# Placing each value of a planned four-layer graph kernel in the buffer that the plan names

## The chip, the cores and the metric

The kernel runs on one core of a Trainium2 chip. A core has engines that work in parallel, each with its own queue of instructions: TensorE (PE, matrix products and transposes; its weight loads are listed apart as PEld), VectorE (DVE), ScalarE (ACT), GpSimd (POOL), and SyncE (SP), which here issues all the DMA transfers. Values lie in SBUF (128 partitions) and, where TensorE writes, in PSUM (8 banks); inputs, the output and a few intermediates lie in HBM. Engines wait for each other through semaphores.

The metric is the device time of one execution in microseconds (us), lower is better. The median of three runs of the kernel before is 2722.01 us (2721.93 to 2723.06).

## The reference

64 graphs of 256 nodes with 256 features, `x` (64, 256, 256), go through four layers, each with the dense weighted adjacency `adj` (64, 256, 256). After each layer comes a residual and a normalisation over the features. Shortened, for one graph, in float32:

```python
# layer 0: 4 heads, sigmoid attention, normalised by the degree
X, q, k = heads(lrelu(x @ W_lin + b_lin)), heads(lrelu(x @ W_q)), heads(lrelu(x @ W_k))
A = adj * sigmoid(q @ k.T * 64 ** -0.5)
deg = A.sum(-1);  dis = where(deg > 0, deg ** -0.5, 0)
x = ln(x + affine_ln((dis[:, None] * A * dis[None, :]) @ X))
# layer 1: 8 heads, softmax attention where adj > 0
s = where(adj > 0, q1 @ k1.T / sqrt(32), NEG)
x = ln(x + heads_joined(softmax(s) @ v1) @ Wo + bo)
# layer 2: sum over neighbours, MLP of width 1024 with an RMS norm and SiLU
h = (eps * x + adj @ x) @ W1 + b1
x = ln(x + silu(h * rsqrt(mean(h ** 2) + 1e-6) * rms_weight) @ W2 + b2)
# layer 3: additive attention, softmax, layer norm, GELU
Wh = x @ W;  e = leaky_relu(s1[:, None] + s2[None, :], 0.2)
x = ln(x + gelu(affine_ln(softmax(where(adj > 0, e, NEG)) @ Wh)))
```

## The kernel before, in words

The program is straight-line code made from a plan. `graph()` (L296) describes one graph's work as a list of operations on named values, for 64 graphs; `weights()` (L225) does the same for the constants. An `Op` (L54) has an engine, an estimated cost, a function that issues its instructions, and the values that it writes and reads. A `Value` (L42) has a kind, which says what it lies in: `s` (128 x 516 words of SBUF, most values), `d` (128 x 1024, the attention weights `e`, `eb`, `eT`), `b` (128 x 2048, `att` and `hT`), `c` (128 x 32, statistics), `p` (one PSUM bank) and `h` (HBM, `far`). `SLOTS` (L39) says how many of each there are at a time: 42, 10, 3, 72, 8 and 8.

`Plan.order()` (L143) is a list scheduler in plain Python that runs when the program is built. It keeps a clock for each engine, takes the operation that can start first, and for each of its new values takes a slot: `self.free[kind]` holds pairs of the time from which a slot is free and its number; it is sorted, and the first is taken (L199, L200). When the last use of a value has been placed, its slot goes back with the time at which that use has landed (L203 to L205). An operation that needs more slots than are free waits until there are enough. So the plan has a slot number, `v.slot`, for each value; but the number goes no further than the plan's own clock. The result is one list, sorted by the planned start (L217), in which operations of up to eight graphs stand beside each other: layers 1, 2 and 3 of a graph run 2, 5 and 7 graphs behind layer 0 (`ROUND`, L37).

`emit()` (L787) goes through that list. It asks a pool for a tile for each value that an operation is the first to use, then issues the operation. Each kind has one pool with as many buffers as `SLOTS` says (L761), and all its tiles have one tag, so the framework beneath decides which of the free buffers a tile gets, by its own account of when each becomes free, and makes the first writer of a tile wait for all readers of the tile that lay there. The framework keeps each engine's instructions in the order in which they are issued (L783); it adds all semaphores.

The steps that the prediction speaks of:

- L434 (VectorE), `y = ps + xb`, the residual after layers 1 and 2, where `ps` comes from L377 or L695; then statistics L391, L393, on POOL L403 and L404, then L414 (VectorE, two numbers per row) and L418 (ScalarE), which makes the next `x1`, `x2` or `x3`.
- L321 (TensorE), the transposes of such an `x`; L377 and L366, products of 256 columns in both layouts.
- L502 (VectorE), `added`, the sum of two halves of `att` (layer 0); L508 (TensorE) sums it over nodes for the degrees; L530 (TensorE) multiplies `att` by the values `v0`.
- L606 (TensorE), `av`, layer 1's attention times `v1`; L623 (VectorE), `yT = av * rb`, where `rb` are the softmax's reciprocals, which come by way of L615 (`rT`, ScalarE), a write to HBM (L616) and eight reads (L619).
- L654 and L656 (ScalarE), `sq` and `hT` of layer 2; L661 and L663 (VectorE) add the `sq`, L668 (TensorE) takes their mean; L695 is the last product of layer 2.
- L333, L339, L343: a transpose by way of HBM (VectorE in blocks, four writes of `far`, four reads), which gives `xT3` (read by L710) and `eT3` (read by L377) in layer 3.

Of the kernel before, what the change touches and what calls it, by code (L numbers as in the profile page):

```python
# [9 lines left out]
F32 = mybir.dt.float32  # L10
# [3 lines left out]
P = 128  # L14
# [15 lines left out]
WORDS = {"s": 516, "d": 1024, "b": 2048, "c": 32, "p": 512, "h": 1024}  # L30
# [8 lines left out]
SLOTS = {"s": 42, "d": 10, "b": 3, "c": 72, "p": 8, "h": 8}  # L39
# [700 lines left out]
@with_exitstack  # L740
def gnn_stack_kernel(ctx: ExitStack, tc: tile.TileContext, t: dict, out: bass.AP):

    nc = tc.nc  # L750
    x_in, xT_in, adj_in, adjT_in = t["x"], t["xT"], t["adj"], t["adjT"]
    B, N, D = x_in.shape
    NB, DB = N // P, D // P
    assert NB == 2 and DB == 2
    H0, H1 = 4, 8
    HD0, HD1 = D // H0, D // H1
    HID = t["L2_gnn_W1"].shape[1]
    HB = HID // P

    const = ctx.enter_context(tc.tile_pool(name="const", bufs=1))  # L760
    pools = {kind: ctx.enter_context(tc.tile_pool(name=f"pool_{kind}", bufs=SLOTS[kind], **(  # L761
        {"space": {"p": bass.MemoryType.PSUM, "h": bass.MemoryType.DRAM}[kind]} if kind in "ph" else {})))
        for kind in SLOTS}


    ident = const.tile([P, P], F32, name="ident")
    make_identity(nc, ident)
    ones = const.tile([P, 32], F32, name="ones")
    nc.vector.memset(ones, 1.0)
    mean_of = const.tile([P, 32], F32, name="mean_of")  # L770
    nc.vector.memset(mean_of, 1.0 / HID)
    mhalf = const.tile([P, 8], F32, name="mhalf")
    nc.vector.memset(mhalf, -0.5)
    c = SimpleNamespace(const=const, ident=ident, ones=ones, mean_of=mean_of, mhalf=mhalf)

    plan = Plan(B)
    weights(plan, nc, c, t)
    for b in range(B):
        plan.graph = b
        graph(plan, nc, c, t, out, b)  # L780
    engines = {mybir.EngineType.PE, mybir.EngineType.DVE, mybir.EngineType.Activation, mybir.EngineType.Pool,
               mybir.EngineType.SP}
    with tc.manual_schedule(engines=engines):  # L783
        emit(plan, pools)


def emit(plan, pools):  # L787
    for op in plan.order():
        for v in op.takes:
            v.full = pools[v.kind].tile([P, WORDS[v.kind]], F32, tag=v.kind, name=v.name)  # L790
            v.t = v.full[:, :512] if v.kind == "s" else v.full
        op.fn()

# [30 lines left out]
```

## Time and profile before

| | us |
|---|---:|
| median of three runs | 2722.01 |
| lowest, highest | 2721.93, 2723.06 |
| the profiled execution | 2723.49 |
| its span, first to last instruction | 2721.6 |
| TensorE busy | 2673.4 |
| VectorE busy | 2441.1 |
| ScalarE busy | 2226.4 |
| GpSimd busy | 595.7 |

The profile is one execution, recorded by the hardware. Busy time is the time in which an engine has an instruction in work. The time from one instruction's start to the next tells more on TensorE, whose instructions overlap. "L502 <- PE L530" in the chain of waits means that the engine sat idle before an instruction of line 502 and that the semaphore which came last was TensorE's, from an instruction of line 530. Which engine or transfer ended a wait is in the profile; whether it was waited for because of a value or because of the room to write to is not, and has to be read from the code. The granted clock of TensorE was 0.996 of full speed over the span, and the 16 DMA engines were busy two thirds of the time (66.2% for the transfers of SP's queue).

### The profile page before, as it was taken

How to read it: one execution, taken by the hardware profiler on the slowest of the kernel's cores; microseconds unless marked ns; L12 is line 12 of the kernel's file. 1: busy time of each engine (PE TensorE's matmuls, PEld its weight loads, DVE VectorE, ACT ScalarE, POOL GpSimd, SP SyncE). 2: the span in 40 equal slices, each digit the busy share in tenths (PEclk: the TensorE clock that was granted, in tenths of full speed). 3: DMA queues.
4: the chain of work that ended last, by engine and by line, in shares of the span. 5: the costliest groups of instructions: out<-in, count | busy, mean ns of one | idle time of the engine just before them, and what ended most of it. 6: DMA issues, size and time to landing. Idle time of an engine off the chain costs nothing.

```text
span 2721.6 us, 56595 instructions
## 1 busy us (share of the span) xinstructions
PE 2673.4 (98%) x17568; PEld 2145.6 (79%) x17568; DVE 2441.1 (90%) x7486; ACT 2226.4 (82%) x5331; POOL 595.7 (22%) x902
## 2 busy tenths in 40 slices
PE   8999999999999999999999999999999999999997
PEld 6777788787887877877878778787778788787776
DVE  6788999899899998999989999989999899999986
ACT  4988788888887888878888788888888888887885
POOL 1111222212222212212222222222222222222212
PEclk9999999999999999999999999999999999999998
DMA  5476876776666766767767677676676676766661
GB/s 150 135 212 176 208 217 164 204 197 183 191 187 181 214 180 181 199 172 208 203 164 206 182 190 213 161 196 193 173 215 188 170 212 184 190 209 177 173 169 38
DMA packets 708045, 501.01 MB, mean 184 GB/s; under 512 B 309792, under 2 KB 667552, under 8 KB 707744
## 3 DMA queue, kind: packets, MB, share of 16 engines
q1 hardware_dynamic: 707744, 497.40, 66.2%
q8 instruction: 140, 2.29, 0.4%
q14 instruction: 161, 1.32, 0.2%
HBM read 301.35 MB, written 195.82 MB: 183 GB/s over the span
## 4 chain that ended last, share of the span: by engine, by line
PE 88%; DVE 4%; ACT 3%; DMA 2%; SPq 1%; issue 1%; POOL 0%; DVEq 0%; POOLq 0%; ACTq 0%
PE ps L366 16%; PE ps L377 15%; PE ps L695 15%; PE ps L649 15%; PE ps L570 5%; PE ps L490 4%; PE ps L530 4%; PE ps L637 4%; PE ps L710 4%; PE av L606 4%; PE ps L321 1%; PE ps L508 1%; ACT e L458 1%; PE pr L681 1%; DVE st L391 1%
## 5 line engine op out<-in xcount | busy, mean ns | idle before, releaser
L458 ACT ACTIVATE e<-e,low 128x256 f32<-128x256 f32 x1152 | 574.7, 500 | 85.2 <-DVE low L453 84.2
L695 PE MATMUL ps<-w,hT 128*128 128x256 f32 x2048 | 466.8, 380 | 1.3 <-ACT hT L687 1.3
L649 PE MATMUL ps<-aggT,w 128*128 128x256 f32 x2048 | 463.4, 380 | 1.6 <-ACT aggT L357 1.0
L695 PEld LDWEIGHTS ps<-w,hT 128*128 128x128 f32 x2048 | 385.7, 190 | 60.4 <-issue 4.6
L649 PEld LDWEIGHTS ps<-aggT,w 128*128 128x128 f32 x2048 | 383.3, 190 | 57.0 <-issue 3.2
L403 POOL TENSOR_SCALAR mv<-mv 128x2 f32<-128x2 f32 x384 | 132.8, 346 | 1347.7 <-DVE mv L393 977.5
L453 DVE CUSTOM_DVE_ANT_0 e<-ps,adj 128x256 f32<-128x256 f32 x1024 | 361.7, 419 | 24.2 <-PE ps L570 24.0
L404 POOL TENSOR_TENSOR mv<-mv,mhalf 128x2 f32<-128x2 f32 x384 | 308.5, 803 | 32.0
L591 DVE STREAM_TRANSPOSE eb<-e 128x1024 f32<-128x1024 f32 x248 | 301.1, 1222 | 0.8 <-ACT e L458 0.7
L656 ACT ACTIVATE hT<-ps,br,r 128x256 f32<-128x256 f32 x512 | 256.0, 585 | 35.0 <-PE ps L695 31.8
L418 ACT ACTIVATE x<-y,mv 128x256 f32<-128x256 f32 x384 | 215.2, 599 | 55.3 <-DVE mv L414 51.6
L654 ACT ACTIVATE sq<-ps,b 128x256 f32<-128x256 f32 x512 | 220.1, 474 | 27.5 <-PE ps L649 23.4
L391 DVE BATCH_NORM_STATS2 st<-y 128x6 f32<-128x256 f32 x640 | 239.0, 410 | 1.2
L458 ACT ACTIVATION_READ_ACCUMULATOR e<-e,low 128x1 f32 x1152 | 219.1, 190 | 0.0
L496 DVE TENSOR_TENSOR att<-att,adjT 128x512 f32<-128x512 f32 x256 | 166.9, 678 | 8.9 <-ACT att L494 8.9
L676 POOL TENSOR_TENSOR rs<-rs,mhalf 128x2 f32<-128x2 f32 x64 | 45.7, 713 | 527.1 <-DVE rs L674 521.6
L516 POOL TENSOR_TENSOR dp<-dp,mhalf 128x8 f32<-128x8 f32 x64 | 109.8, 1715 | 214.6 <-DVE dp L515 168.4
L685 DVE TENSOR_TENSOR hT<-hT,pr 128x1024 f32<-128x1024 f32 x128 | 150.0, 1211 | 5.3 <-PE pr L681 4.5
L570 PE MATMUL ps<-kT,qT 32*128 32x256 f32 x2048 | 148.2, 400 | 0.0
L661 DVE TENSOR_TENSOR sq<-sq 128x512 f32<-128x512 f32 x192 | 130.0, 677 | 13.0 <-ACT sq L654 12.0
L366 PE MATMUL ps<-x0T,w_q 128*128 128x256 f32 x512 | 130.4, 385 | 6.3 <-DMA x0T<-in_xT 6.3
L494 ACT ACTIVATE att<-ps 128x512 f32<-128x512 f32 x256 | 132.2, 602 | 3.9 <-PE ps L490 3.2
(114 smaller groups left out, 5515.5 us busy)
## 6 DMA issues: line engine op xcount, KB each, us to landing
far<-eb SPq DMA_DIRECT2D x248, 512.0 KB, 3.6
eT<-far SPq DMA_DIRECT2D x992, 128.0 KB, 4.1
adj<-in_adj SPq DMA_DIRECT2D x128, 256.0 KB, 5.0
far<-eb SPq DMA_DIRECT2D x488, 64.0 KB, 2.0
x0T<-in_xT SPq DMA_DIRECT2D x64, 256.0 KB, 4.6
adjT<-in_adjT SPq DMA_DIRECT2D x64, 256.0 KB, 5.1
x<-in_x SPq DMA_DIRECT2D x64, 256.0 KB, 5.2
adj<-in_adjT SPq DMA_DIRECT2D x64, 256.0 KB, 4.7
```

Of the source, the lines that this page charges most:

```text
L366: pe.matmul(two(ps)[:, o, :], w.t[:, k, o * P:(o + 1) * P], two(xT)[:, k, :], start=(k == 0), stop=(k == DB - 1))
L377: pe.matmul(two(ps)[:, n, :], two(xT)[:, k, n * P:(n + 1) * P], w()[:, k, :], start=(k == 0), stop=(k == DB - 1))
L391: op("DVE", 328, lambda n=n: dve.bn_stats(st.t[:, 6 * n:6 * n + 6], two(src)[:, n, :]), [(st, n)], [(src, n)])
L404: pool.tensor_tensor(m()[:, :, 2], m()[:, :, 2], c.mhalf[:, :NB], OP.pow)
L453: op("DVE", 345, lambda n=n: dve.tensor_tensor_reduce(out=E(n), in0=two(logits)[:, n, :], in1=two(negmask)[:, n, :], scale=-scale, scalar= ...
L458: op("ACT", 491, lambda n=n: act.activation(E(n), E(n), AF.Exp, bias=low.t[:, n:n + 1], scale=-1.0, accum_out=r.t[:, col(n):col(n) + 1]), ...
L570: pe.matmul(two(pss[i])[:, n, :], two(qT1)[s, hq, n * P:(n + 1) * P], two(kT1)[s, hq, :], start=True, stop=True)
L591: op("DVE", 1155, lambda e=e, eb=eb: dve.transpose(eb.t.rearrange("p (b g i) -> p g b i", b=4, i=32), e.t.rearrange("p (g b i) -> p g b i" ...
L649: pe.matmul(two(ps)[:, i, :], c.w2_1.t[:, k, (j + i) * P:(j + i + 1) * P], two(aggT)[:, k, :], start=(k == 0), stop=(k == DB - 1))
L654: op("ACT", 357, lambda ps=ps, sq=sq, i=i, j=j: act.activation(two(sq)[:, i, :], two(ps)[:, i, :], AF.Square, bias=c.b2_1.t[:, j + i:j + i ...
L656: op("ACT", 491, lambda ps=ps, i=i, j=j: act.activation(Hb(j + i)[:, 0], two(ps)[:, i, :], AF.Identity, bias=c.br2.t[:, j + i:j + i + 1], ...
L695: pe.matmul(two(ps)[:, n, :], Hb(j)[:, 0, n * P:(n + 1) * P], c.w2_2.t[:, j, :], start=(j == 0), stop=(j == HB - 1))
```

## The change

Each pool now gives out single buffers, one for each tag, and the tag holds the plan's slot number. So there are 42 tags `s0` to `s41`, ten `d0` to `d9`, and so on; a value lies in the buffer whose number the plan gave it, and its first writer waits for the readers of the value that had this number before. The number of buffers of each kind and their sizes stay as they are.

```diff
-    pools = {kind: ctx.enter_context(tc.tile_pool(name=f"pool_{kind}", bufs=SLOTS[kind], **(
+    pools = {kind: ctx.enter_context(tc.tile_pool(name=f"pool_{kind}", bufs=1, **(
         {"space": {"p": bass.MemoryType.PSUM, "h": bass.MemoryType.DRAM}[kind]} if kind in "ph" else {})))
         for kind in SLOTS}
...
 def emit(plan, pools):
+
     for op in plan.order():
         for v in op.takes:
-            v.full = pools[v.kind].tile([P, WORDS[v.kind]], F32, tag=v.kind, name=v.name)
+            v.full = pools[v.kind].tile([P, WORDS[v.kind]], F32, tag=f"{v.kind}{v.slot}", name=v.name)
             v.t = v.full[:, :512] if v.kind == "s" else v.full
         op.fn()
```

## The prediction

> **What bounds the kernel now.** First the page's busy times.
>
> ```profile
> PE 2673.4 (98%) x17568; PEld 2145.6 (79%) x17568; DVE 2441.1 (90%) x7486; ACT 2226.4 (82%) x5331; POOL 595.7 (22%) x902
> ```
>
> TensorE sets the end. A busy PE is not yet a full one, so I looked at the distance from matmul to matmul: 215 to 216 ns for each 256-column record, hardly ever more. What can be won is the idle time between them: PE is busy 91.3 of the first 100 us, 2480.8 of the 2500 us after it (the table by stretches), and idle 20.7 us of the end. The middle loses 19.2 us, and that is all a change of buffers can give there. Next the chain of waits for PE alone: waiter, what ended the wait, us in total, times, longest.
>
> ```profile
> PE ps L366 <- DMA x0T<-in_xT: 6.3, 1, 6.3
> PE ps L321 <- ACT x L418: 5.6, 10, 1.0
> PE ps L377 <- DVE mv L393: 2.9, 10, 0.4
> PE ps L321 <- DVE y L434: 2.3, 5, 0.5
> PE ps L508 <- DVE added L502: 2.2, 5, 0.4
> PE ps L668 <- DVE sq L663: 1.8, 1, 1.8
> ```
>
> The first is the start's load. The next four are one pattern: six small stalls, 2.6 us together, that return every 334 us (8 graphs) between 534 and 2036 us, five times over. Why is the engine that PE waits for late? The waits of VectorE tell it:
>
> ```profile
> DVE y L434 <- PE av L606: 11.3, 9, 1.6
> DVE yT L623 <- PE ps L530: 9.7, 7, 1.5
> DVE added L502 <- PE ps L377: 9.6, 5, 1.9
> DVE added L502 <- PE ps L530: 5.8, 5, 1.2
> DVE added L502 <- DMA out<-o: 3.2, 1, 3.2
> ```
>
> None of these five is for data. L502 adds two halves of `att`; L434 adds `ps` (of L695 or L377) and `xb`; L623 multiplies `av` and `rb`. The releaser is each time the last reader of whatever lay in the buffer that the result is written to: the waits are for room. One of them in order of time (start, duration, in brackets the idle time before):
>
> ```profile
> 864.35 0.42 DVE L663 TENSOR_TENSOR sq<-sq 128x256 f32<-128x256 f32 x1
> 865.58 0.69 DVE L434 TENSOR_TENSOR y<-ps,xb 128x512 f32<-128x512 f32 x1 [0.81 <-PE av L606]
> 867.43 0.69 DVE L502 TENSOR_TENSOR added<-att 128x512 f32<-128x512 f32 x1 [1.17 <-PE ps L530]
> ```
> ```profile
> 868.18 0.43 PE L508 MATMUL ps<-added,ones 128*32 128x128 f32 x8 [0.44 <-DVE added L502]
> 868.54 0.66 PE L321 MATMUL ps<-ident,x 128*128 128x128 f32 x4
> 869.59 1.75 PE L377 MATMUL ps<-w_o,yT 128*128 128x256 f32 x7 [0.40 <-DVE mv L393]
> ```
>
> VectorE waits 1.98 us for room, and PE then 0.84 us for VectorE.
>
> **What the Trainium skill says.** Perfetto Trace Analysis, Optimization Strategy: a gap that repeats on the engine that should be saturated can mean that there is not enough SBUF or PSUM for the next tile. The five returns agree, with one difference: room there was, only not the room that was picked. Perfetto Trace Analysis, Tensor Engine Instruction: ACT and DVE are strict FIFO. The trace agrees: whatever stands behind a held L502 starts after it. The same page, Identifying Dependency Chains: an instruction that waits on several engines gets semaphore instructions ahead of it; so another set of waits changes their number. SBUF — State Buffer, "SBUF: two separate sides": between engines only the GpSimd/Vector port is shared. So a value's place should not change an operation's time; no run here shows it yet.
>
> **The change part by part.** Nothing is computed differently, and each engine's order is written out by the plan, so every instruction and DMA keeps its place in its queue. What moves is which value lies where, hence who waits for whose last reader. (1) *Which takeovers change.* The plan hands out the slot that by its clock has been free longest (the sorted `free` list in `order`). I listed its slots and set the trace's times beside them. Of 7491 takeovers in SBUF and PSUM, 2345 get another former value: 1429 in pool s, 326 in d, 377 in p, 213 in c, none in b. The `far` values (h) lie in HBM; by the plan's slots the closest reuse leaves 15.6 us, so they cost nothing.
>
> (2) *What goes.* The stalls with the plan's former value:
> - 868.18 and 869.59: y takes over from an xb last read at 859.91, `added` from an aggT last read at 860.19. y can start at 864.69 (the operation before is done), `added` at 865.30 and end at 866.0; its matmul wants it at 867.74. yT follows `added` by 1.36 us as now: 866.66 to 867.3, wanted at 868.75. Both stalls go: 0.84 us.
> - 948.64 and 950.31: y waits from 946.2 to 947.80; its new slot is free since 944.20. It ends at 946.9, wanted at 948.17; yT, held next by the end of av at 947.8, ends at 948.5, wanted at 949.66. 0.65 us.
> - 1033.82 and 1034.3: `added` waits from 1030.1 to 1032.03 for the reader of a yT; its new slot (an adj) is free since 1024.91. The small mv of L414 behind it, now at 1032.98, can start at 1031.05, ACT's L418 after the two hT at 1031.33, and the halves of x1 end by 1031.9 and 1032.4; PE wants them at 1032.86. 0.96 + 0.17 = 1.13 us.
>
> Sum 2.61 us, five times: 13.0 us, which is also the sum of the four rows (5.6 + 2.9 + 2.3 + 2.2). The L668 row comes once, at 2466 us: ACT's sq at 2460.11 stood 1.91 us for the write of rT to HBM; its new slot, a qT1, is free since 2457.30, before ACT gets there at 2458.1. 1.8 us. Together 14.8 us.
>
> (3) *What is added.* In the unchanged trace only six takeovers would come before the last read of the former value, by 0.00 to 1.95 us, 3.99 us in all. Four are SP's `eT` transfer (L343) at 699.84, 1033.73, 1366.79 and 1701.09, after an xb that L434 reads: this L434 stands behind the held L502 of the last stall, so it moves 1.9 us earlier, and more than the 0.00 to 1.02 us needed. Were that cover gone, SP would hold, and the `rb`, `far` and `eT` transfers behind it; these four `eT` are used 5.2 to 6.1 us after they land. One is an `rb` piece at 292.98 (1.95 us; first use 23.7 us after landing). One is ACT's kT1 at 2451.52 (0.41 us, with L570 a microsecond away). Taken as nothing; the other end is all 3.99 us on PE.
>
> (4) *Waits.* PE's own semaphore instructions will differ in number. The 16 matmuls of L490 take 1.62 us with none, one or two of them in between, those of L570 0.77 us: nothing. On DVE (972 now) one shows 21 to 50 ns; a hundred more or fewer are 5 us of DVE, which idles 280: nothing on PE.
>
> (5) *Stalls that stay*: 4.4 us of the middle (hT at 207.5, yT by DMA at 181.1, xT at 1133, 1801 and 2135, some singles), which take the same slots or wait for data; the start and the end.
>
> The profiled execution took 2723.5 us, of which 1.9 lie outside its span of 2721.6; minus 14.8 that is 2708.7. The median of the runs is 1.5 us below it: 2722.0 - 14.8 = 2707.2.
>
> **The rivals.** *No wait goes* (8%): the waits I read as room are ordering that stays, or the slots picked come out alike: 2722. For it only that the releasers are inferred; against it that the code gives L502 nothing to read from L377 or L530.
>
> *Another wait takes the place* (10%): behind the stalls at 1033.8 stands ACT's L656, idle 35 us in all for hT, whose three buffers rotate as before. If it holds x1 by more than the 0.9 us to spare, those 5.65 us stay: 2712.8. If PE, earlier by 2.6 us a period, also meets its `xT` (L710), which lands as little as 0.25 us ahead of use, half of the rest goes too: 2717.4, within what can be told.
>
> *Slower* (6%): the plan's clock is not the chip's. Once the stalls go, transfers come earlier, and SP, one queue, may be held for room where I see none. The price is 1.02 us (the worst of the four) at one `eT`; the `xT` transfers behind it have 0.25 us, so 0.77 us reach PE per graph. Held in 26 graphs it eats 14.8 + 5.4 us and is slower; in all 61: 2707.2 + 47 = 2754. Against it: four holds in 61, none ahead of a tight xT.
>
> **How the numbers follow.** A kernel like this one, with runs within 1.1 us, can tell about 0.2% (5.4 us): below 2716.6 is faster, above 2727.4 slower. My forecast has 76%: from 2702 (the last 4.4 us of the middle go too) to 2713. With the first part of the second rival this fills 2702 to 2716.5, 81%. Faster 0.82 (forecast and that part); same 0.12 (no wait goes, or most gain is given back); slower 0.06.
>
> **What would show it.** Right: the four rows of PE's waits fall from 13.0 to under 3 us, L668's goes, L502's waits for PE (15.4 us) disappear, as do those of L434 for av; PE busy stays 2673 in a span of about 2707; hT's 35 us on ACT stay. Wrong: new rows for SP at L343 with DVE L434, or PE waiting at L710 or L377 for `eT`; or per-operation times that moved with the addresses.

## The result, and the profile after

The changed kernel takes 2696.15 us (median of six runs, 2694.70 to 2699.38) where the kernel before takes 2721.76 us beside it (six runs, 2718.05 to 2723.06). The ratio is 0.9909, with a 95% interval of 0.9896 to 0.9922. A second set of runs (`after_again`), with the kernel before on the same chip, gave 2698.15 against 2721.07: 0.9917 (0.9902 to 0.9932). The change makes the kernel 23 to 26 us faster. The forecast was 2707.2 us: the direction is right, and the gain is nearly twice the one forecast; the time lies below the range.

The profiled execution of the changed kernel took 2699.38 us. Its page begins so (span; busy time, share and instructions of each engine):

```profile
span 2697.6 us, 56490 instructions
...
PE 2664.2 (99%) x17568; PEld 2144.8 (80%) x17568; DVE 2440.3 (90%) x7486; ACT 2224.6 (82%) x5331; POOL 591.5 (22%) x902
```

Every engine executes as many instructions as before; the whole program has 105 fewer, which are semaphore instructions. The span fell by 24.0 us, from 2721.6 to 2697.6. Two subtractions from this page and the one before split it. The time in which PE is *not* busy, span less PE, fell from 48.2 to 33.4 us: 14.8 us. But PE's *busy* time fell too, from 2673.4 to 2664.2 us, for the same 17568 matmuls: 9.2 us. The forecast has the first part and not the second.

The waits of PE in the changed kernel (waiter, what ended the wait, us in total, times, longest):

```profile
PE ps L366 <- DMA x0T<-in_xT: 6.6, 1, 6.6
PE ps L366 <- ACT xT L357: 1.4, 1, 1.4
PE ps L695 <- ACT hT L687: 1.3, 2, 1.1
PE ps L649 <- ACT aggT L357: 1.0, 2, 0.7
PE ps L710 <- ACT xT L357: 1.0, 1, 1.0
PE ps L649 <- DVE low L453: 1.0, 2, 0.6
PE ps L321 <- ACT e L458: 1.0, 2, 0.7
PE ps L710 <- DMA xT<-far: 0.8, 1, 0.8
```

The rows L377 for mv, L321 for y and L508 for added of the five-fold pattern and the row of L668 are gone, the row L321 for x fell from 5.6 to 0.2 us (one wait near the end), and only waits that occur once or twice are left. VectorE's waits show why. `added` (L502) no longer waits for anything. What y and yT wait for is now the matmul whose result they read (besides the rows below, L695 for y, and one wait of 0.5 us for an `rb` transfer):

```profile
DVE yT L623 <- PE av L606: 19.9, 16, 2.5
...
DVE y L434 <- PE ps L377: 10.9, 14, 1.7
```

The stall that the prediction followed instruction by instruction (864 to 870 us before) lies at 858 to 864 us now. VectorE and then PE, in order of time:

```profile
857.98 0.41 DVE L663 TENSOR_TENSOR sq<-sq 128x256 f32<-128x256 f32 x1
858.32 0.68 DVE L434 TENSOR_TENSOR y<-ps,xb 128x512 f32<-128x512 f32 x1
858.92 0.68 DVE L502 TENSOR_TENSOR added<-att 128x512 f32<-128x512 f32 x1
```
```profile
861.08 0.65 PE L508 MATMUL ps<-added,ones 128*32 128x128 f32 x16
861.66 0.66 PE L321 MATMUL ps<-ident,x 128*128 128x128 f32 x4
862.15 1.89 PE L377 MATMUL ps<-w_o,yT 128*128 128x256 f32 x8
```

VectorE has no bracket (no idle time) left, `added` ends 1.5 us before its matmul starts, and the sixteen L508 are one uninterrupted group. Now take the distance between two starts instead of the brackets. The first eight L508 of the kernel before:

```profile
867.32 0.43 PE L508 MATMUL ps<-added,ones 128*32 128x128 f32 x8
```

From there to L377 at 869.59 it was 2.27 us. Now it is 861.08 to 862.15: 1.07 us. So 1.20 us came back, where the brackets showed 0.44 + 0.40 = 0.84. The difference is 0.18 us for each of the two stalls. This is the first sign of what the forecast missed.

### The profile page after: what moved, and what is told of

Read it like the earlier page. It is cut to its first block, busy times and chain, and to the rows that moved or that the text cites. A ratio compares the mean times of both kernels' runs of the same rounds, so it can differ in the third digit from the quotient of the medians.

```text
span 2697.6 us, 56490 instructions
## 1 busy us (share of the span) xinstructions
PE 2664.2 (99%) x17568; PEld 2144.8 (80%) x17568; DVE 2440.3 (90%) x7486; ACT 2224.6 (82%) x5331; POOL 591.5 (22%) x902
## 4 chain that ended last, share of the span: by engine, by line
PE 94%; DVE 2%; ACT 2%; DMA 1%; issue 0%; SPq 0%; POOL 0%; POOLq 0%; DVEq 0%; ACTq 0%
PE ps L366 16%; PE ps L695 16%; PE ps L377 16%; PE ps L649 15%; PE ps L570 5%; PE ps L490 4%; PE ps L530 4%; PE av L606 4%; PE ps L710 4%; PE ps L637 4%; PE ps L321 1%; PE ps L508 1%; PE pr L681 1%; PE ps L719 0%; DVE e L453 0%
## 5 line engine op out<-in xcount | busy, mean ns | idle before, releaser
L695 PE MATMUL ps<-w,hT 128*128 128x256 f32 x2048 | 466.8, 380 | 1.3 <-ACT hT L687 1.3
L649 PE MATMUL ps<-aggT,w 128*128 128x256 f32 x2048 | 463.4, 380 | 2.0 <-ACT aggT L357 1.0
L695 PEld LDWEIGHTS ps<-w,hT 128*128 128x128 f32 x2048 | 385.7, 190 | 60.4 <-issue 4.6
L649 PEld LDWEIGHTS ps<-aggT,w 128*128 128x128 f32 x2048 | 383.3, 190 | 57.4 <-issue 2.5
L453 DVE CUSTOM_DVE_ANT_0 e<-ps,adj 128x256 f32<-128x256 f32 x1024 | 361.7, 419 | 30.3 <-PE ps L570 30.1
L656 ACT ACTIVATE hT<-ps,br,r 128x256 f32<-128x256 f32 x512 | 256.1, 586 | 34.3 <-PE ps L695 31.1
L418 ACT ACTIVATE x<-y,mv 128x256 f32<-128x256 f32 x384 | 215.1, 600 | 27.3 <-DVE mv L414 25.2
L570 PE MATMUL ps<-kT,qT 32*128 32x256 f32 x2048 | 145.7, 399 | 0.0
L366 PE MATMUL ps<-x0T,w_q 128*128 128x256 f32 x512 | 130.4, 385 | 6.6 <-DMA x0T<-in_xT 6.6
```

Of the source, the lines that this page charges most:

```text
L366: pe.matmul(two(ps)[:, o, :], w.t[:, k, o * P:(o + 1) * P], two(xT)[:, k, :], start=(k == 0), stop=(k == DB - 1))
L453: op("DVE", 345, lambda n=n: dve.tensor_tensor_reduce(out=E(n), in0=two(logits)[:, n, :], in1=two(negmask)[:, n, :], scale=-scale, scalar= ...
L570: pe.matmul(two(pss[i])[:, n, :], two(qT1)[s, hq, n * P:(n + 1) * P], two(kT1)[s, hq, :], start=True, stop=True)
L649: pe.matmul(two(ps)[:, i, :], c.w2_1.t[:, k, (j + i) * P:(j + i + 1) * P], two(aggT)[:, k, :], start=(k == 0), stop=(k == DB - 1))
L656: op("ACT", 491, lambda ps=ps, i=i, j=j: act.activation(Hb(j + i)[:, 0], two(ps)[:, i, :], AF.Identity, bias=c.br2.t[:, j + i:j + i + 1], ...
L695: pe.matmul(two(ps)[:, n, :], Hb(j)[:, 0, n * P:(n + 1) * P], c.w2_2.t[:, j, :], start=(j == 0), stop=(j == HB - 1))
```

## The experiments

Where an experiment's lines are numbered otherwise than the changed kernel's, the text says so. Ratios are to the kernel before on the same chip. Unless it is said, a kernel computes all of the reference.

### Does naming the buffers do anything by itself?

`e1_named_as_before`: one named buffer per number, as in the changed kernel, but a table gives each value the buffer in which it lay before.

```diff
...
     for op in plan.order():
         for v in op.takes:
+            if v.kind in PLACED:
+                v.slot, count[v.kind] = ord(PLACED[v.kind][count[v.kind]]) - 48, count[v.kind] + 1
             v.full = pools[v.kind].tile([P, WORDS[v.kind]], F32, tag=f"{v.kind}{v.slot}", name=v.name)
```

> Every value has a named buffer, as in the change, but the buffer is the one that the kernel before gave it. Theory A (the gain is the placement alone: who waits for whose last reader): the time is that of the kernel before, 2722 us within 5, with the same five-fold pattern of stalls and 'DVE added L502 <- PE ps L377' near 9.6 us. Theory B (named buffers help by themselves, through fewer semaphores or a simpler wait): below 2710 us.

Measured: 2720.69 us, ratio 0.9997 (0.9990 to 1.0003). The four rows of the pattern are those of the kernel before (L668 waits 1.1 us here, and 1.8 us before):

```profile
PE ps L321 <- ACT x L418: 5.6, 10, 1.0
PE ps L377 <- DVE mv L393: 2.9, 10, 0.4
PE ps L321 <- DVE y L434: 2.3, 5, 0.5
PE ps L508 <- DVE added L502: 2.2, 5, 0.4
```

The form of the pools is worth nothing that these times can tell. The gain lies in which value takes over from which. Here too the program has 56595 instructions, as before: their number follows the placement, not the names. That leaves a rival, that fewer semaphore instructions make the gain; two runs further down speak against it. `e6_just_freed` has 56851 instructions, 256 more than the kernel before, and is 18 us faster than it; `e3_all_but_s` has 56548, 47 fewer, and is no faster.

### Which pool carries it?

`e2_s_only` names the buffers of pool s alone; `e3_all_but_s` names those of d, b, c, p and h, and leaves s pooled. The edit of e2 (e3 has "dbcph" for "s"):

```diff
-bufs=1, **(
+bufs=1 if kind in "s" else SLOTS[kind], **(
...
-tag=f"{v.kind}{v.slot}"
+tag=f"{v.kind}{v.slot}" if v.kind in "s" else v.kind
```

> Plan's slots in pool s alone; in d, b, c and p the framework picks from a shared pool, as before. Theory A (the false waits of y, added and yT, all in pool s): nearly the whole gain, 2694 to 2702 us. Theory B (a part of the gain beyond the predicted 14.8 us comes from PSUM slots, p, where L570 waited 2 us at 296 us): about 10 us of it missing, 2704 to 2710 us.

> The complement: plan's slots in d, b, c and p, a shared pool for s. Theory A: 2717 to 2724 us, nothing gained beyond a few us. Theory B (PSUM slots matter): 2708 to 2714 us.

Measured: s alone 2702.19 us, 0.9918 (0.9902 to 0.9935); all but s 2721.36 us, 0.9993 (0.9984 to 1.0001), with the same four rows of PE waits as before, 5.6, 2.9, 2.3 and 2.2 us. So pool s carries the gain, within the interval all of it, and the 916 takeovers that differ in d, c and p are worth nothing without it that the times can tell (e3's trace lacks two stalls of PE near 208 us, 1.3 us together). s alone brings one new row of several waits, six times at most 0.4 us, which the whole change doesn't have:

```profile
PE ps L377 <- ACT rT L615: 2.3, 6, 0.4
```

### Is it the three values that were held?

`e4_three_only`: the placement of before, except that y, added and yT of pool s get a buffer that by the plan has been free for over 1 us, the one that is next needed latest (and the two buffers swap their later values). Of the 7491 takeovers in SBUF and PSUM 115 differ from before.

```diff
...
+        if v.name not in ("y", "added", "yT"):
+            continue
...
+        room = [i for i, u in holds.items() if ends[u] < n and u.end < order[n].start - 1000]
+        if room:
+            best, own = max(room, key=lambda i: then.get(i, 1 << 30)), at[v]
+            for _, u in takes[j:]:
+                at[u] = {best: own, own: best}.get(at[u], at[u])
...
```

> The placement of the kernel before, except that the values named y, added and yT get a slot that has been free for a microsecond or more by the plan's clock; 115 of 7491 takeovers differ from the kernel before. Theory A: this handful of waits carries the gain; the stall at L668 (1.9 us) may stay: 2696 to 2702 us. Rival (the gain is spread over many small waits, of which these are only the visible ones): 2706 to 2714 us.

Measured: 2703.19 us, 0.9923 (0.9909 to 0.9938): 1.2 us above the range expected and 2.8 us below the rival's, so the time alone doesn't part them. The trace does: its waits lose the pattern.

```profile
PE ps L366 <- DMA x0T<-in_xT: 6.2, 1, 6.2
...
PE ps L710 <- DMA xT<-far: 1.4, 3, 0.6
PE ps L668 <- DVE sq L663: 1.0, 1, 1.0
PE ps L649 <- ACT aggT L357: 1.0, 2, 0.7
PE ps L377 <- DVE mv L393: 1.0, 1, 1.0
```

PE's matmuls stand in the same order in all these kernels, so their starts can be set side by side, one by one. Over its five returns the pattern takes 18.9 us less in e4 than in the kernel before, as it does in the changed kernel; in e1 and e3 it takes as long as before, within 0.1 us. So 115 takeovers bring some 20 of the 25 us, and the cause named in the prediction is the cause of the pattern: three results of VectorE that were written into a buffer whose last reader had not come by yet. Which of the three is needed wasn't tried.

### The opposite choice

`e5_three_just_freed`: the changed kernel, but y, added and yT take the free buffer that was released last in the order of issue.

```diff
...
+            if v.name in ("y", "added", "yT") and v.kind == "s":
+                free = [i for i, u in enumerate(holds["s"]) if u is None or ends[u] < n]
+                other = max(free, key=lambda i: -1 if holds["s"][i] is None else ends[holds["s"][i]])
...
```

> The changed kernel, except that the values named y, added and yT get the slot that became free last in the order of issue. Set beside the times of the changed kernel, 277 of these takeovers would come before the former value's last read, by 304 us in all, against 58 us for the placement of the kernel before. Theory A (a takeover costs by how late its room is): slower than the kernel before, 2750 to 2830 us. Rival (such waits hide behind TensorE's queue beyond the six places already seen): 2715 to 2740 us.

Measured: 2880.49 us, 1.0582 (1.0567 to 1.0598), 50 us above the range expected. The instructions of each engine stand in the same order as before; three kinds of values lie elsewhere:

```profile
span 2884.4 us, 56497 instructions
...
PE 2728.4 (95%) x17568; PEld 2165.2 (75%) x17568; DVE 2450.2 (85%) x7486; ACT 2225.1 (77%) x5331; POOL 606.5 (21%) x902
```

PE's greatest wait, and two of VectorE's, for a transfer that still reads the buffer:

```profile
PE ps L377 <- DVE yT L623: 39.8, 21, 3.6
```
```profile
DVE yT L623 <- DMA far<-eb: 45.1, 14, 4.3
...
DVE y L434 <- DMA out<-o: 39.8, 16, 3.7
```

Against the changed kernel the idle time of PE (span less busy) grew from 33.4 to 156.0 us, 122.6 us; and PE's busy time grew by 64.2 us for the same matmuls. A third of this loss is in no bracket. The busy time is thus no constant of the instructions, while the forecast treated it as one.

### Longest free, or free by a good clock?

`e6_just_freed`: in the plan, of the buffers that are free by its clock when an operation starts, the one released *last* is taken, not the first. (Lines after L200 are one higher.)

```diff
-                v.slot = self.free[v.kind].pop(0)[1]
+                last = max(sum(when <= start for when, _ in self.free[v.kind]) - 1, 0)
+                v.slot = self.free[v.kind].pop(last)[1]
```

> The changed kernel, except that the plan takes, among the slots free by its own clock, the one freed last instead of the one freed first. Set beside the times of the changed kernel 102 takeovers come too early, by 37.7 us in all, none by design. Theory A1 (what matters is that the slot is taken from the one free longest): as bad as the kernel before or worse, 2720 us or more. Theory A2 (what matters is that the plan's clock is near the chip's, so that a slot which it holds free is free): 2698 to 2712 us.

Measured: 2704.47 us, 0.9933 (0.9918 to 0.9947). Reversing the rule that the prediction gave weight to (the buffer that has been free longest) costs 6 to 8 us of the 25 and no more. What counts is that the buffer is free at all when its turn comes, and the plan's clock is near enough to the chip's for that; how near it must be wasn't tried. In e5 the last-released buffer was chosen by order of issue, which knows no time; here it was chosen by the plan's time, and little was lost.

### What does one stall of PE cost?

The rest of the work is on the 9 us that the forecast missed. The trace of before has 53 idle times of at least 0.1 us ahead of a matmul, that of after 19, so 34 fewer. If each costs 0.17 us beside its bracket (the idle time that the profile shows before it), they make 5.8 us. To measure the price by itself I put into each of the 64 graphs, after the matmuls of L508, one VectorE operation on their result (into z, a tile of its own) and one small matmul, in two arrangements; what the reference wants is computed as before. In `e7_matmul_free` the matmul reads a constant and was meant not to wait; in `e8_matmul_held` it reads what VectorE has written. (Lines after L511 are two higher in these and in the next two.)

```diff
+        dve.tensor_tensor(c.z, ps.t[:, :P], c.ident, OP.mult)
+        pe.matmul(ps.t[:32, N:N + P], c.ones, c.ident, start=True, stop=True)   # e7
+        pe.matmul(ps.t[:32, N:N + P], c.ones, c.z, start=True, stop=True)       # e8
```

> The changed kernel with two instructions more per graph after L508: a VectorE product of the result's first 128 columns with a constant into a tile of its own, and one small matmul of 128 columns that reads a constant and waits for neither. It is the base line for the next run: 64 x 0.2 us of TensorE and what VectorE loses by waiting for L508, 2705 to 2740 us; no idle time of TensorE at the small matmul.

> As the run before, but the small matmul reads the VectorE tile, so that TensorE stands still 64 times until VectorE has answered. Theory P (a stall costs the idle time that the profile shows plus about 0.17 us of overlap between matmuls that is lost, as 3.7 us came back where the profile had shown 2.6): the time above the base line exceeds the idle time added on TensorE by 64 x 0.12 to 0.2, 8 to 13 us. Rival Q (a stall costs what the profile shows): by 0 to 3 us.

Measured: 2751.38 us, 1.0105 (1.0090 to 1.0121), and 2752.04 us, 1.0109 (1.0093 to 1.0126). The pair tells nothing apart, since the baseline waits as well. In e7 this row stands among PE's waits, though the matmul doesn't read z:

```profile
PE ps L511 <- DVE z L510: 30.5, 64, 1.1
```

It writes other columns of the same PSUM tile that VectorE is reading, and is made to wait for that reader, 0.48 us per matmul.

So the baseline was made anew: in `e10_matmul_first` the matmul with the constant stands *ahead* of the VectorE operation, where it waits for nothing; `e11_matmul_held` is e8 again, run beside it.

```diff
+        pe.matmul(ps.t[:32, N:N + P], c.ones, c.ident, start=True, stop=True)
+        dve.tensor_tensor(c.z, ps.t[:, :P], c.ident, OP.mult)
```

> The extra matmul of the two runs before it, and the extra VectorE product, in the other order: the matmul follows L508 at once and waits for nobody. In the run meant as a base line the matmul writes the PSUM bank that VectorE is reading, so it waited 64 times as well (30.5 us idle in all) and the two did not differ. Theory P (a stall costs its idle time plus about 0.17 us of lost overlap): the held kernel lies above this one by its added idle time and 64 x 0.12 to 0.2 us more, 37 to 44 us. Rival Q (a stall costs what the profile shows): by 28 to 32 us.

> The held matmul again, on the chip of the run before: 2752 us within 5.

Measured: 2718.63 us, 0.9990 (0.9981 to 0.9999), and 2750.78 us, 1.0110 (1.0095 to 1.0125). The groups of the added matmul (busy and mean; idle before and its releaser), first of e10 and then of e11:

```profile
L510 PE MATMUL ps<-ident,ones 128*32 128x128 f32 x128 | 24.4, 273 | 0.0
```
```profile
L511 PE MATMUL ps<-z,ones 128*32 128x128 f32 x128 | 26.0, 285 | 30.6 <-DVE z L510 30.6
```

And the pages of the two, the busy time of the engines, again first e10 (span 2715.4 us) and then e11 (span 2748.8 us):

```profile
PE 2678.8 (99%) x17696; PEld 2154.1 (79%) x17696; DVE 2452.3 (90%) x7550; ACT 2224.8 (82%) x5331; POOL 590.0 (22%) x902
```
```profile
PE 2687.5 (98%) x17696; PEld 2152.2 (78%) x17696; DVE 2455.7 (89%) x7550; ACT 2223.8 (81%) x5331; POOL 590.7 (21%) x902
```

The span grows by 33.4 us. Idle time (span less PE) grows from 36.6 to 61.3 us, 24.7 us; PE's busy time grows by the other 8.7 us, with 17696 matmul records in both. e11 has 77 idle times of at least 0.1 us and e10 has 28, so 49 more: 8.7 / 49 = 0.18 us for each, beside its bracket. The medians lie 32.2 us apart, below the 37 to 44 us expected and at the edge of the rival's 28 to 32, so the times alone would have spoken for the rival. Both expectations took the 30.6 us of e11's row as all new, while e10 has some stalls that e11 lacks, so that only 24.7 us of idle time were added. At the place itself nothing is mixed in: from the start of the last L508 to the start of the matmul that follows the added one, the 64 passages take 25.2 us in e10 and 69.1 us in e11. That is 43.9 us more, where the row shows 30.6 us of idle time: 0.21 us for each beside its bracket. So a stall costs about 0.2 us more than its idle time here, and the rival, that idle time is the whole price, falls.

### A wait that stays: hT's three buffers

`e9_four_b`: pool b, in which hT lies and for which ACT's L656 waits, gets four buffers instead of three, and c sixteen fewer.

```diff
-SLOTS = {"s": 42, "d": 10, "b": 3, "c": 72,
+SLOTS = {"s": 42, "d": 10, "b": 4, "c": 56,
```

> The changed kernel with one buffer more of kind b (four instead of three, for att and hT) and 56 instead of 72 of kind c, which are never short. ScalarE's 34 us of waiting at L656 for the last reader of a former hT should nearly go. Theory A (ScalarE's waits there cost nothing, TensorE is busy meanwhile): 2691 to 2699 us. Rival (they delay sq and hT, and through them TensorE): 2680 to 2690 us.

Measured: 2711.86 us, 0.9968 (0.9956 to 0.9979): about 14 us slower than the changed kernel beside it, which neither theory expected. Its list of PE's waits has two new rows, for `att`:

```profile
PE ps L695 <- ACT att L494: 2.7, 2, 1.9
PE ps L366 <- ACT att L494: 2.2, 1, 2.2
```

With other numbers of buffers the planner writes another order for every engine, so this compares two plans and not three buffers with four. Whether hT's wait costs anything in the order at hand wasn't tried. No version here beats the changed kernel.

## Where the prediction was right, and the step that failed

**Which waits go: right.** The stalls at 868, 948 and 1034 us and their four returns are gone, and so are the four rows (13.0 us), L668 and every wait of L502. e1 shows that the placement is the cause, e2 and e3 that it lies in pool s, and e4 that y, added and yT are enough for most of it. One stretch of 500 us, in which parts of two returns lay, from the table by stretches (its time; then PE, PEld, DVE, ACT and POOL busy), of before and of after:

```profile
1000.00:1500.00 500.00, 496.08 (x3271) 399.49 (x3268) 455.99 (x1389) 414.99 (x987) 113.62 (x168) 1.00 0.70 190
```
```profile
1000.00:1500.00 500.00, 500.00 (x3302) 404.14 (x3301) 461.45 (x1415) 419.61 (x1003) 114.26 (x170) 1.00 0.69 191
```

PE now has no idle time in this stretch at all, where 3.92 us had been to win. The matmuls that lay in it before take 5.8 us less now from start to start.

**Nothing takes their place: right.** L656's wait for hT stays (31.8 us before, 31.1 after), and it holds x1 no longer. PE has no wait for an `eT` transfer. The stall at the xT transfers moved: from start to start 1.5 us at 1133, 1801 and 2135 us went, and 1.7 us came at 627, 957 and 1947 us. One new wait of 0.56 us stands at 107.6 us (L649 for DVE's low). The waits of y, added and yT are for data now.

**The size: wrong, and this is the step that failed.** Under "what goes", each stall was priced at the idle time that the trace has in brackets: 2.61 us a period, 1.8 for L668. And PE's busy time was to stay at 2673 us. From start to start the period's six stalls were 3.77 us and not 2.61, hence 18.9 us and not 13.0 over the five: 0.19 us for each stall beside its bracket. The reason shows in the lines: a matmul of 256 columns has a recorded length of 379 ns, while the next starts 216 ns after it. A matmul that waits starts after the recorded end of the one before, a matmul that doesn't starts 163 ns ahead of it, and this overlap is what the bracket leaves out. It isn't the same everywhere. At L668 and L681, whose matmuls start 309 and 203 ns after the one ahead when nothing holds them, it was 0.07 us; at the L377 of 869.59 us, 0.24 us, of which 0.07 us are the first matmul after the stall, recorded with 454 ns in place of 382. The Trainium skill, Perfetto Trace Analysis, Tensor Engine Instruction (MATMUL, LD_WEIGHTS), says that the end of a matmul in the profile is estimated and not observed; the trace agrees in that recorded ends lie 163 ns behind the next start.

That idle time fell by just the 14.8 us forecast is in part luck: the pattern and L668 gave 14.9 us, and of what the forecast had left as it was 1.8 us went (L681, three xT and small ones) and 1.9 us came (L649, two xT, the first load and small ones).

The same thing shows in one stall with no bracket at all. PE at 296 us, before and after:

```profile
295.63 3.16 PE L570 MATMUL ps<-kT,qT 32*128 32x256 f32 x16
```
```profile
294.27 1.15 PE L570 MATMUL ps<-kT,qT 32*128 32x256 f32 x16
```

These are the same sixteen matmuls. Before, they waited for PSUM room, which VectorE's L453 had to make, and L453 was late behind `added` (L502), held 3.2 us by `DMA out<-o`; the delay is gone in e2 and e4 as well, and it stays in e3, where s is pooled. The prediction showed that very row of VectorE's waits and gave it no price, as no bracket on PE answered to it. It cost 2.0 us. L570 at 210 us was 0.6 us faster too, but not for this cause: there VectorE waited 1.31 us for L570, and in e2, e3 and e4 this delay went or stayed together with the stall of L681 at 207.5 us. In the groups by line, L570's busy time fell from 148.2 to 145.7 us.

**"That is all a change of buffers can give there": wrong.** The 19.2 us of idle time in the middle were taken for an upper bound. What came back there is 23.9 us from start to start, and the range ended at the idle time.

**"Stalls that stay": one was wrong.** The stall at 207.5 us (L681 for hT) went as well, 0.71 us. It was put down to data or an unchanged buffer, while L681 reads nothing that L656 writes: this wait was for PSUM room. It is gone in e3 as well, where pool p is placed, but also in e2, where it is not, so which takeover removed it stays open.

The sum from the records, start to start: the five-fold pattern 18.9; L668 1.9; L570 2.0 + 0.6; L681 0.7; the start 0.8; less 0.2 by which the xT stalls grew and 0.5 for L649. That is 24.2 of the 24.4 us by which all pairs of starts shrank; the first matmul, which waits for x0T, started 0.3 us later, and so the span fell by 24.0 us. The 0.8 us of the start are no effect of the change that I can show: PE ran at half its clock for 6.8 us there before and for 3.4 us after, and e1 and e6 have no such stretch there.

**The six late takeovers and the number of semaphore instructions: nothing, as taken.** 105 fewer, of which 49 on PE; e6 with 256 more than the kernel before is as fast as e4. The new places moved no operation's duration: L695 has 466.8 us in 2048 records both before and after, and among all groups of over 20 instructions (by line, operation and tile) no median moved by more than 6 ns.

Two sums of the prediction are a little off, without effect: the 20.7 us of idle time at the end take in 0.4 us beyond the span, and 26 graphs at 0.77 us make 20.0 us, not 20.2.

## What to carry to other kernels

Where the matmul engine is saturated, price a stall from the start of one matmul to the start of the next, in the place with the stall and in a place without it; the idle time between them is a lower bound, here 0.07 to 0.24 us short per stall, and a stall can be all inside a group that reads as busy. Look in the code whether the releaser of a wait makes what the waiter reads: if it doesn't, the wait is for room, and another choice among the same buffers can remove it for nothing. Which of the free buffers is taken matters less than that it is free on the chip when its turn comes: the opposite rule by the plan's clock (e6) lost 6 to 8 of the 25 us, while a choice for three values that knows no time (e5) cost 180 us.

## What the runs showed of the hardware that I had not expected

PE's busy time isn't fixed by its instructions: 2664.2, 2673.4 and 2728.4 us for the same 17568 records. The last figure, of e5, has a second part beside the overlaps. One stall of it, PE in order of time:

```profile
538.66 3.45 PE L377 MATMUL ps<-w_o,yT 128*128 128x256 f32 x8 [2.85 <-DVE yT L623]
542.04 1.15 PE L570 MATMUL ps<-kT,qT 32*128 32x256 f32 x16
```

And the table by stretches around it; the third figure from the end is the granted clock:

```profile
535.20:538.60 3.40, 0.61 (x9) 0.09 (x1) 0.78 (x2) 0.26 (x1) 0.00 (x0) 0.95 0.33 63
538.60:542.00 3.40, 3.34 (x8) 2.53 (x8) 2.83 (x17) 3.11 (x13) 0.00 (x0) 0.55 0.39 63
542.00:545.40 3.40, 3.40 (x49) 2.16 (x48) 2.14 (x10) 2.01 (x9) 0.00 (x0) 1.00 0.49 77
```

After 2.85 us of idle time the eight L377 take 3.45 us at about half the clock; in the changed kernel the same eight take 1.89 us without a stall. e5 has 20 stretches at half clock, 85.1 us with those at the start and the end, where the changed kernel has 17.6 us. By estimate half of the difference, some 34 us, is lost by them, and 131 more stalls at 0.17 us make 22 us: together 56 of the 64.2 us by which the busy time grew. The Trainium skill, TensorE: Matmul & The Clock Gate, "What's actually happening", says that the clock falls to a half after an idle window of some 3.4 us, and that the windows run free. The stretches of e5 agree in two points: between its start and its end they last 3.41 us or twice that, and their starts lie whole multiples of 3.41 us apart. In the idle time they differ: here a bracket of 2.85 us preceded one. No window has to be wholly idle: each stretch of e5 begins after a window of this grid in which PE is recorded busy for 1.73 us or less, about half of it (four more such windows after its start were not followed by one). That the stall causes the slow stretch is seen only from their order in time; no run here varied the length of a stall by itself.

In the two profiled executions compared above it plays no part, since neither has such a stretch between its start and its end. But the stalls that the change removes are long enough for it. e3, which keeps the stalls at 296 and 2466 us of the kernel before, has a stretch of 3.41 us at half clock behind each, the second after a bracket of 1.94 us; the eight L366 behind it take 3.65 us there, and 1.99 us in the kernel before. How often this happens in executions that weren't profiled isn't known.
